# A gated feed-forward layer with quantised activations: down_w rounded by two ScalarE activations, maxima over four slots, tokens scaled in one VectorE step

## The chip, the cores and the metric

The kernel runs on one core of one Trainium2 chip. A core has five engines with a queue each, which work in order and wait for one another through semaphores: TensorE (PE in the profile, with its weight loads as PEld), VectorE (DVE), ScalarE (ACT), GpSimd (POOL) and SyncE (SP), which here issues nearly all DMAs. The metric is the device time of one execution in microseconds (us).

## The reference

The input is x (4 batches of 1024 tokens, 512 features), a condition vector per batch, norm_w, up_w (4096 x 512) and down_w (512 x 2048). Cut to what matters:

```python
scale = cond @ norm_w.T + 1.0
ms = mean(x * x, axis=-1)
h = x * (scale[:, None, :] * rsqrt(ms + EPS))
val, gate = split(h @ up_w.T, 2, axis=-1)
h = val * gelu(gate)
hq = act_quant(h)        # per token: round(h * 127 / max|h|), clipped, scaled back
wq = weight_quant(down_w)  # clip(round(w / mean|w|), -1, 1), scaled back
y = hq @ wq.T + x
```

So down_w becomes a matrix of -1, 0 and 1 with one factor, and each token of h needs the largest absolute value over all 2048 hidden features before it can be quantised.

## The kernel before

The four batches run one after the other. The 2048 hidden features are 16 blocks of 128; a batch does block j = 0 to 15, each in two halves h = 0, 1 of 512 tokens. The order of all work is written out by hand (a manual schedule), and each engine's queue follows it.

The product with up_w is done in float16 pairs (a high and a low part). In the first batch it is done plainly: `plain_half(j, h)` (lines 606 to 614) issues 12 matmuls for the gate into a PSUM bank (pg), the Gelu on ACT (L610), 12 matmuls for the value (pv, bank "E", of which there are two), and on DVE the multiplication of both into H (L614). With two banks, pv of a half can start only when L614 of the half before last has emptied its bank. The later batches use a fast product (`product`, L571) with fewer multiplications, on weights that the first batch has prepared.

So the first batch also carries, between its halves, all that prepares the rest. For each block, in `first_batch(j, sc)`: the row-wise range of up_w (`w_range`: L277, L147, L283, L286, and `w_gain` L292, on DVE), its scaling (`w_scale`, L304 on ACT), its split in two (`w_rows`: L328 on ACT, L329 on DVE, then a transposing DMA by SP), the sums of weight blocks (`s_sums`, L362 to L365 on POOL), their split (`s_high` L374 on ACT, `s_low` L378 on POOL), and the write of all this to DRAM (`s_spill`).

Three things more are spread over its blocks by small tables:

- down_w lies in R[:, 1] in eight parts of 128 x 1024. `d_sum` (ACT) has summed them, `d_total` (L437) and `d_mean` (L442 to L444, with one small matmul, pmean) make the mean and its reciprocal wsc. `d_round(n)` scales, clips to -1 and 1 and rounds part n by adding MAGIC = 1.5 * 2^23, in two DVE steps (L448, L449); `d_put(n)` takes MAGIC off again on ACT and writes fp8 (L458), and after every second part SP issues a transposing DMA (L460). `D_ROUND` says in which block.
- the tokens of the second batch (class `Tokens`, b == 1), four groups of 256 tokens, begun in blocks 6, 8, 10 and 12 (`TOKENS`): `norm` sums squares on ACT (L505), POOL makes rs (L475, L476), `scale` multiplies by rs on ACT (L513, twice) and by the condition's row sc on DVE (L518), `sums` are four POOL steps (L526 to L529). In the next block `high` (L550, ACT), `low` (L554, DVE) and `turn` (a transposing DMA, L557) follow.
- the largest absolute h per token for batch 0: `pair_max(0, i, h)` takes the maximum over blocks 2i and 2i + 1 (`tensor_reduce` over two slots, 1024 elements a partition, L700 or L705) and, but for the first pair, folds it into the running maximum (L707). `PAIRS` says in which block.

Parts of down_w, the second batch's transposed tokens and the running maxima share R: a group's `turn` writes over parts of down_w, so these must have been rounded by then.

Of the kernel before, what the change touches and what calls it, by code (L numbers as in the profile page):

```python
# [8 lines left out]
F32 = mybir.dt.float32  # L9
# [4 lines left out]
AF = mybir.ActivationFunctionType  # L14
ALU = mybir.AluOpType
# [3 lines left out]
P = 128  # L19
EXPONENT = 0x7F800000  # L20
MAGIC = 1.5 * 2.0**23
# [29 lines left out]
def glu_quant_kernel(  # L51
# [10 lines left out]
    PE, ACT, DVE, POOL, SP = nc.tensor, nc.scalar, nc.vector, nc.gpsimd, nc.sync  # L62
    B, S, D = x.shape
# [6 lines left out]
    NJ = FF // P  # L70
# [4 lines left out]
    cpool = ctx.enter_context(tc.tile_pool(name="const", bufs=1))  # L75
# [4 lines left out]
    ident = cpool.tile([P, P], F32, name="ident")  # L80
    neghalf = cpool.tile([P, 4], F32, name="neghalf")
    DVE.memset(neghalf, -0.5)
    one = cpool.tile([P, 1], F32, name="one")
    DVE.memset(one, 1.0)
    ones = one.to_broadcast([P, P])
# [36 lines left out]
    def m_view(b, h):  # L122
        return R[:, b % 2, M_AT + TOK * h : M_AT + TOK * (h + 1)]
# [16 lines left out]
    def h_slots(g, n=1):  # L140
        s = g % NSLOT
        return H[:, s : s + n]
# [73 lines left out]
    def cond_spread(dg, b0, b1, tag):  # L216
        n = b1 - b0
        pd = bank(tag, {"po": 3}.get(tag, 2), [P, B], f"pd_{b0}")[:, :n]
        PE.matmul(pd, ones[:n, :], dg, start=True, stop=True)
        return pd  # L220

    def cond_undo(pd, b0, b1):
        DVE.reciprocal(ux[:, b0:b1], pd)
        if b0 == 0:
            DVE.tensor_scalar(scT[:, :, 0], scT[:, :, 0], ux[:, 0:1], None, ALU.mult)
        DVE.tensor_copy(dx[:, b0:b1], pd)
# [40 lines left out]
    def w_load(j, ts=(1, 0)):  # L267
        if j > 2:
            SP.dma_start(out=wn(j), in_=up_v[j])
            return  # L270
        for t in ts:
            SP.dma_start(out=wn(j)[:, t], in_=up_v[j][:, t])
# [15 lines left out]
    def w_range(j, t0=0, t1=2):  # L288
        w_factor(j, w_largest(j, t0, t1), t0, t1)

    def w_gain(j):
        DVE.tensor_scalar(sg0[:, j, :], sw[:, j, :], dx[:, 0:1], None, ALU.mult)  # L292
# [63 lines left out]
    def s_sums(j):  # L356
        if j >= ROWS:
            v = wn(j).rearrange("p t (n f) -> p t n f", n=2)
            a11, a12, a21, a22 = v[:, 1, 0], v[:, 1, 1], v[:, 0, 0], v[:, 0, 1]
        else:  # L360
            a11, a12, a21, a22 = (wf(j)[:, n] for n in range(4))
        POOL.tensor_tensor(sf[:, 0], a21, a22, ALU.add)  # L362
        POOL.tensor_tensor(sf[:, 2], a11, a21, ALU.subtract)
        POOL.tensor_tensor(sf[:, 1], sf[:, 0], a11, ALU.subtract)
        POOL.tensor_tensor(sf[:, 3], a12, sf[:, 1], ALU.subtract)  # L365
# [49 lines left out]
    wsc = cpool.tile([P, 1], F32, name="wsc")  # L415
# [4 lines left out]
    def d_part(n):  # L420
        return R[:, 1, n * HF : (n + 1) * HF]

    def d_at(n):

        return n // 4 + 2 * (n % 2), n // 2 % 2, n % 2
# [9 lines left out]
    def d_total():  # L435
        part = sm.tile([P, 1], F32, name="wpart", bufs=1)
        DVE.tensor_reduce(part, wsum, AX.X, ALU.add)  # L437
        return part
# [5 lines left out]
        DVE.reciprocal(wsc, wmean)  # L444

    def d_round(n):
        dn = d_part(n)
        DVE.tensor_scalar(dn, dn, wsc, 1.0, ALU.mult, ALU.min)  # L448
        DVE.tensor_scalar(dn, dn, -1.0, MAGIC, ALU.max, ALU.add)  # L449

    tn = []

    def d_put(n):
        _, u, y = d_at(n)
        if y == 0:
            tn.append(wpool.tile([P, HF], BF16, name=f"tn_{n}", tag="v"))
        t8 = tn[-1].bitcast(F8).rearrange("p (f y) -> p f y", y=2)
        ACT.activation(t8[:, :, y], d_part(n), AF.Copy, bias=-MAGIC, saturate=False)  # L458
        if y:
            SP.dma_start_transpose(wd[:, n // 4, u], tn[-1])  # L460

# [16 lines left out]
    class Tokens:  # L478
# [31 lines left out]
        def scale(self, sc):  # L510
            xn, xt = self.xn, self.xt
            for h in range(2):
                ACT.activation(xn[:, h], xn[:, h], AF.Copy, scale=self.rs[:, h : h + 1])  # L513
                if self.b > 1:
                    POOL.tensor_tensor(xn[:, h], xn[:, h], sc, ALU.mult)
            if self.b == 1:
                s2 = sc.rearrange("p (o d) -> p o d", o=1).to_broadcast([P, 2, D])
                DVE.tensor_tensor(xn, xn, s2, ALU.mult)  # L518
            if self.b > 1:
                self.sums()  # L520

# [84 lines left out]
    def plain_half(j, h, between=nothing):  # L606
        pg = bank(*(("A", 2) if h or j == 1 else ("B", 1)), name=f"pg_{j}_{h}")
        plain(j, 1, h, pg)
        t1 = wpool.tile([P, TOK], F32, name=f"g_{j}_{h}", tag="t1")
        ACT.activation(t1, pg, AF.Gelu, scale=gain(j, 1))  # L610
        between()
        pv = bank("E", 2, name=f"pv_{j}_{h}")
        plain(j, 0, h, pv)
        DVE.scalar_tensor_tensor(h_half(j, h), pv, gain(j, 0), t1, ALU.mult, ALU.mult)  # L614
# [77 lines left out]
        z()  # L692


    def pair_max(b, i, h):

        v = h_slots(b * NJ + 2 * i, 2)[:, :, h].rearrange("p j t -> p t j")
        m = m_view(b, h)
        if i == 0:
            return [lambda: DVE.tensor_reduce(m, v, AX.X, ALU.max, apply_absolute_value=True)]  # L700
        gm = []

        def largest():
            gm.append(wpool.tile([P, TOK], F32, name=f"gm_{b}_{i}_{h}", tag="gm", bufs=1))
            DVE.tensor_reduce(gm[0], v, AX.X, ALU.max, apply_absolute_value=True)  # L705

        return [largest, lambda: DVE.tensor_tensor(m, m, gm[0], ALU.max)]  # L707
# [286 lines left out]
    def second_part():  # L994
# [8 lines left out]


    D_SUM = {0: (4, 5), 1: (6, 7), 2: (2, 3), 3: (0, 1)}
    D_ROUND = {4: (0, 1), 5: (2,), 6: (3, 4), 8: (5, 6), 10: (7,)}
    D_MEAN = min(D_ROUND)
    TOKENS = {6: 0, 8: 1, 10: 2, 12: 3}
    PAIRS = {
        3: [(0, 0), (0, 1)], 4: [(1, 0), (1, 1)], 6: [(2, 0)], 7: [(2, 1)],  # L1010
        14: [(3, 0), (3, 1), (4, 0), (4, 1)], 15: [(5, 0), (5, 1), (6, 0), (6, 1)],
    }
    toks = {}

    def next_tokens(j):

        if j in TOKENS:
            toks[j] = toks[j + 1] = Tokens(1, TOKENS[j])
            toks[j].load()
# [6 lines left out]
    def first_batch(j, sc):  # L1026

        if j + 2 <= LATE:
            w_load(j + 4)
        if j >= 4:  # L1030
            next_tokens(j + 2)
        t = toks.get(j)
        odd = t is not None and j not in TOKENS
        n = j + 2
        rows = LATE <= n < NJ
        if j + 1 < LATE:
            s_sums(j + 1)
        elif rows:
            s_sums(n)
        if j + 3 < NJ:  # L1040
            w_range(j + 3)
            w_gain(j + 3)
        if j == D_MEAN:
            part = d_total()
        plain_half(j, 0)
        if j == 3:
            pd = cond_spread(dg, 1, B, "po")
            cond_undo(pd, 1, B)
            cond_rows()
        pairs = PAIRS.get(j, ())  # L1050
        for i, h in pairs[:2]:
            for f in pair_max(0, i, h):
                f()
        if n < LATE:
            w_scale(n)
            w_rows(n)
        if j + 1 < LATE:
            s_all(j + 1)
        if t and not odd:
            t.norm()  # L1060
        for m in D_ROUND.get(j - 1, ()):
            d_put(m)
        for m in D_ROUND.get(j, ()) if j > D_MEAN else ():
            d_round(m)
        if t and not odd:
            t.scale(sc)
            t.sums()
        if j + 2 > LATE and j + 5 < NJ:
            w_load(j + 5)
        if odd:  # L1070
            t.high()
            t.low(DVE)
        if odd:
            t.turn()
        plain_half(j, 1)
        if j == D_MEAN:
            d_mean(part)
        own = rows and j + 1 >= LATE
        if own:
            s_high(n)  # L1080
            s_low(n, POOL)
        if LATE <= j + 3 < NJ:
            w_scale(j + 3)
            w_rows(j + 3)
        if own:
            s_spill(n)
        elif rows:
            s_sums(n)
            s_all(n)
            w_load(j + 5)  # L1090
        for m in D_ROUND[j] if j == D_MEAN else ():
            d_round(m)
        for i, h in pairs[2:]:
            for f in pair_max(0, i, h):
                f()
        for n in D_SUM.get(j, ()):
            d_sum(n)
        if j in (NJ - 3, NJ - 1):
            s_load_x(NJ + (j - NJ + 3) // 2)
            s_load_y(NJ + (j - NJ + 3) // 2)  # L1100
# [81 lines left out]
    for j in range(3, NJ):  # L1182
        if j == 5:
            sc = cond_load_scale(1)
# [90 lines left out]
    for b in range(1, B):  # L1275
# [5 lines left out]
        for h in range(2):  # L1281
            add_pair(
                dve, act, b - 1, last_pair, h, (0, "xz"[h]),
                lambda now, h=h: token_max(b - 1, h, am),
# [9 lines left out]
        pairs = {}  # L1294
        if b + 1 < B:
            sc = cond_load_scale(b + 1)
# [109 lines left out]
    b = B - 1  # L1406
# [159 lines left out]
```

## Time and profile before

| what | value |
|---|---|
| median of 3 runs | 735.0 us (734.93 to 735.55) |
| the profiled execution | 735.1 us |
| its span, first to last instruction | 733.3 us |
| PE busy | 721.2 us (98%) |
| DVE busy | 600.6 us (82%) |
| ACT busy | 390.9 us (53%) |
| POOL busy | 200.1 us (27%) |
| granted clock of PE | 1.00 throughout |

How to read it: the span is divided in stages with quite different loads. From 0 to about 44 us the first data come in and blocks 0 to 2 are begun; from 50.5 to 190.3 us blocks 3 to 15 of the first batch run, two halves each; after that the three other batches follow. Busy shares of the whole span say little about one stage, so the stage with the change in it has to be looked at by itself, and an engine's idle time counts only where it is on the chain that ends last. The lines of the rows are those of the kernel before.

### The profile page before, as it was taken

The page shows a single profiled execution, that of the slowest core. Times are in us where ns is not written, and L with a number is a line of the kernel's source. Part 1 is how long each engine was busy: PE and PEld are TensorE (multiplying, and loading weights), DVE is VectorE, ACT ScalarE, POOL GpSimd, SP SyncE. Part 2 cuts the span into 40 slices and gives each one's busy share as a digit, 9 for nine tenths or more (in the row PEclk, how much of TensorE's full clock was granted, in tenths as well). Part 3 has the DMA queues.
Part 4 walks back from the last instruction along what each step waited for, and adds up shares of the span by engine and source line. Part 5 has one row for each costly group of instructions (what it writes and reads, how often), then busy time and mean ns, then how long its engine had stood idle before and what let it go on. Part 6 is the DMA issues. An engine that isn't in the chain of part 4 may idle for free.

```text
span 733.3 us, 10144 instructions
## 1 busy us (share of the span) xinstructions
PE 721.2 (98%) x3661; PEld 358.5 (49%) x3661; DVE 600.6 (82%) x828; ACT 390.9 (53%) x629; POOL 200.1 (27%) x207
## 2 busy tenths in 40 slices
PE   7999999999999999999999999999999999999998
PEld 3544444444444445655444445666444444445744
DVE  6979999787898899797689887787678888755897
ACT  6868657664235675435335666453433665332274
POOL 1379867886200032450010030461020000000100
PEclk9999999999999999999999999999999999999999
DMA  6759989998344645866844646766934455452253
GB/s 239 245 176 284 275 232 237 263 260 217 116 99 103 133 107 170 180 161 173 205 101 102 123 107 173 180 145 166 227 97 105 95 110 104 102 104 91 87 188 114
DMA packets 203982, 117.30 MB, mean 160 GB/s; under 512 B 165382, under 2 KB 174487, under 8 KB 203932
## 3 DMA queue, kind: packets, MB, share of 16 engines
q1 hardware_dynamic: 203642, 116.33, 62.6%
q8 instruction: 28, 0.46, 0.3%
q10 hardware_dynamic: 290, 0.33, 0.1%
q14 instruction: 22, 0.18, 0.1%
HBM read 54.22 MB, written 23.09 MB: 105 GB/s over the span
## 4 chain that ended last, share of the span: by engine, by line
PE 84%; DVE 9%; ACT 2%; issue 2%; POOL 1%; DMA 1%; SPq 0%; DVEq 0%; ACTq 0%
PE A L571 34%; PE E L571 17%; PE B L571 8%; PE po L842 8%; PE pv L586 5%; PE pg L586 5%; PE po_end L791 4%; DVE H L614 1%; DVE H L329 1%; DVE wam L277 1%; PE po L791 1%; DVE R L448 1%; DMA H<-in_x_dram 1%; DVE gm L705 1%; DVE nx L554 1%
## 5 line engine op out<-in xcount | busy, mean ns | idle before, releaser
L571 PEld LDWEIGHTS <-SXY 128*128 128x128 f16 x2016 | 197.0, 98 | 232.5 <-issue 0.6
L571 PE MATMUL A<-R,SXY 128*128 128x512 f16 x1152 | 266.3, 379 | 0.0
L571 PE MATMUL E<-R,SXY 128*128 128x512 f16 x576 | 140.0, 379 | 0.1
L669 DVE SCALAR_TENSOR_TENSOR H<-A,sg,t 128x512 f32<-128x512 f32 x48 | 36.0, 750 | 73.2 <-PE A L571 73.1
L721 POOL PARTITION_ALL_REDUCE am<-R x8 | 14.3, 1793 | 232.0 <-DVE R L707 232.0
L763 DVE TENSOR_TENSOR H<-H,am 128x1024 f32<-128x1024 f32 x64 | 76.3, 1218 | 0.0
L586 PEld LDWEIGHTS <-SXY 128*128 128x128 f16 x486 | 47.4, 98 | 59.0 <-issue 1.7
L682 ACT ACTIVATE t<-t,sg 128x512 f32<-128x512 f32 x48 | 34.6, 721 | 70.2 <-DVE t L679 70.1
L571 PE MATMUL B<-R,SXY 128*128 128x512 f16 x288 | 70.0, 379 | 0.0
L705 DVE TENSOR_REDUCE gm<-H 128x512 f32<-128x1024 f32 x56 | 69.0, 1231 | 1.0
L586 PE MATMUL pg<-R,SXY 128*128 128x512 f16 x252 | 57.8, 379 | 0.3 <-DMA SXY<-H 0.3
L842 PE MATMUL po<-wd,R 128*128 128x256 fp8e4 (+1 forms) x448 | 56.8, 275 | 0.0
L586 PE MATMUL pv<-R,SXY 128*128 128x512 f16 x234 | 54.4, 379 | 1.1 <-DVE H L614 1.1
L842 PEld LDWEIGHTS <-R 128*128 128x128 bf16 (+1 forms) x480 | 46.9, 98 | 12.9
L666 ACT ACTIVATE t<-B,sg 128x512 f32<-128x512 f32 x48 | 33.0, 687 | 35.9 <-PE B L571 35.9
L475 POOL TENSOR_SCALAR ssq<-ssq 128x2 f32<-128x2 f32 x12 | 3.6, 299 | 176.7 <-ACT xt L505 124.1
L649 ACT COPY t<-A 128x512 f32<-128x512 f32 x48 | 27.9, 582 | 39.8 <-PE A L571 39.5
L657 ACT COPY B<-A 128x512 f32<-128x512 f32 x48 | 27.5, 572 | 39.0 <-PE A L571 38.6
L771 ACT ACTIVATE H<-H 128x1024 f32<-128x1024 f32 x38 | 39.9, 1050 | 14.2 <-DVE H L763 14.1
L661 ACT COPY v<-E 128x512 f32<-128x512 f32 x48 | 28.1, 585 | 31.6 <-PE E L571 27.8
L707 DVE TENSOR_TENSOR R<-R,gm 128x512 f32<-128x512 f32 x56 | 41.8, 747 | 1.3
L688 DVE SCALAR_TENSOR_TENSOR H<-v,sg,t 128x512 f32<-128x512 f32 x48 | 36.6, 762 | 7.4 <-ACT t L682 7.4
(206 smaller groups left out, 992.7 us busy)
## 6 DMA issues: line engine op xcount, KB each, us to landing
SXY<-s_dram SPq DMA_DIRECT2D x57, 256.0 KB, 3.1
s_dram<-SXY SPq DMA_DIRECT2D x18, 384.0 KB, 3.2
H<-in_L_cond_up_w_dram SPq DMA_DIRECT2D x13, 512.0 KB, 5.1
SXY<-s_dram SPq DMA_DIRECT2D x39, 128.0 KB, 3.2
xr<-in_x_dram SPq DMA_DIRECT2D x19, 256.0 KB, 3.1
out_dram<-xr SPq DMA_DIRECT2D x19, 256.0 KB, 2.5
H<-in_x_dram SPq DMA_DIRECT2D x8, 512.0 KB, 7.6
R<-in_L_cond_down_w_dram SPq DMA_DIRECT2D x8, 512.0 KB, 6.7
```

The costliest lines, as they stand in the source:

```text
L571: PE.matmul(o, s[:, w, k, :], tv[:, :, c, l, k, :], start=start and n == 0, stop=stop and n == len(TERMS) - 1, skip_group_check=True,)
L586: PE.matmul(ps, a[k // 2][:, w, k % 2, :], XP[:, l, k, h * TOK : (h + 1) * TOK], start=n == 0, stop=n == len(terms) - 1,)
L666: ACT.activation(cur["t1"], pb, AF.Gelu, scale=gain(g, 1))
L669: DVE.scalar_tensor_tensor(h_half(g - 1, 0), prev["A"], gain(g - 1, 0), prev["t1"], ALU.mult, ALU.mult)
L682: ACT.activation(prev["t2"], prev["t2"], AF.Gelu, scale=gain(g - 1, 1))
L688: DVE.scalar_tensor_tensor(h_half(g - 1, 1), prev["v"], gain(g - 1, 0), prev["t2"], ALU.mult, ALU.mult)
L705: DVE.tensor_reduce(gm[0], v, AX.X, ALU.max, apply_absolute_value=True)
L707: return [largest, lambda: DVE.tensor_tensor(m, m, gm[0], ALU.max)]
L763: DVE.tensor_tensor(v, v, r.to_broadcast([P, 2, TOK]), ALU.mult)
L771: ACT.activation(v, v, AF.Copy, bias=MAGIC)
L791: PE.matmul(po.rearrange("p (y c o) -> p y c o", c=2, o=P), q[:, a, h, j], wd8[:, :, j // n, j % n, :, y0:y1].rearrange("p c o y -> p y c o"),
L842: PE.matmul(po, w[:, j], m, start=start and j == 0, stop=stop and j == n - 1, skip_group_check=True,)
```

## The change

It has three parts, all within the first batch:

1. `d_round` becomes one ACT activation (Copy with scale wsc and bias MAGIC, which rounds), and `d_put` uses the function Sign with bias -MAGIC in place of Copy, which maps the rounded integer to -1, 0 or 1. Both stand together in the half before the second one of a block; the parts are spread over blocks 5, 6, 7, 9, 10, 11 and 12. A constant tile `unmagic` is set at the start.
2. For the second batch, `Tokens.scale` no longer uses ACT: DVE does `(x * rs) * sc` in one step for each of the two rows.
3. `pair_max` can take several pairs at once; three of the four calls for each half now reduce over four slots (2048 elements a partition), and the table `LARGEST` has one call in a block.

```diff
+    unmagic = cpool.tile([P, 1], F32, name="unmagic")
+    DVE.memset(unmagic, -MAGIC)
...
     def d_round(n):
         dn = d_part(n)
-        DVE.tensor_scalar(dn, dn, wsc, 1.0, ALU.mult, ALU.min)
-        DVE.tensor_scalar(dn, dn, -1.0, MAGIC, ALU.max, ALU.add)
+        ACT.activation(dn, dn, AF.Copy, scale=wsc, bias=MAGIC)
...
-        ACT.activation(t8[:, :, y], d_part(n), AF.Copy, bias=-MAGIC, saturate=False)
+        ACT.activation(t8[:, :, y], d_part(n), AF.Sign, bias=unmagic, saturate=False)
...
             for h in range(2):
-                ACT.activation(xn[:, h], xn[:, h], AF.Copy, scale=self.rs[:, h : h + 1])
-                if self.b > 1:
+                r = self.rs[:, h : h + 1]
+                if self.b == 1:
+                    DVE.scalar_tensor_tensor(xn[:, h], xn[:, h], r, sc, ALU.mult, ALU.mult)
+                else:
+                    ACT.activation(xn[:, h], xn[:, h], AF.Copy, scale=r)
                     POOL.tensor_tensor(xn[:, h], xn[:, h], sc, ALU.mult)
-            if self.b == 1:
-                s2 = sc.rearrange("p (o d) -> p o d", o=1).to_broadcast([P, 2, D])
-                DVE.tensor_tensor(xn, xn, s2, ALU.mult)
...
-    def pair_max(b, i, h):
+    def pair_max(b, i, h, pairs=1):
-        v = h_slots(b * NJ + 2 * i, 2)[:, :, h].rearrange("p j t -> p t j")
+        v = h_slots(b * NJ + 2 * i, 2 * pairs)[:, :, h].rearrange("p j t -> p t j")
...
-    D_ROUND = {4: (0, 1), 5: (2,), 6: (3, 4), 8: (5, 6), 10: (7,)}
-    D_MEAN = min(D_ROUND)
+    D_ROUND = {5: (0, 1), 6: (2,), 7: (3,), 9: (4,), 10: (5,), 11: (6,), 12: (7,)}
+    D_MEAN = 4
-    PAIRS = {
-        3: [(0, 0), (0, 1)], 4: [(1, 0), (1, 1)], 6: [(2, 0)], 7: [(2, 1)],
-        14: [(3, 0), (3, 1), (4, 0), (4, 1)], 15: [(5, 0), (5, 1), (6, 0), (6, 1)],
+    LARGEST = {
+        4: (0, 0, 2), 5: (0, 1, 2), 8: (2, 0, 2), 10: (2, 1, 2), 12: (4, 0, 2), 13: (4, 1, 2),
+        14: (6, 0, 1), 15: (6, 1, 1),
     }
...
-        pairs = PAIRS.get(j, ())
-        for i, h in pairs[:2]:
-            for f in pair_max(0, i, h):
+        if j in LARGEST:
+            for f in pair_max(0, *LARGEST[j]):
                 f()
...
-        for m in D_ROUND.get(j - 1, ()):
+        for m in D_ROUND.get(j, ()):
+            d_round(m)
             d_put(m)
-        for m in D_ROUND.get(j, ()) if j > D_MEAN else ():
-            d_round(m)
...
-        for m in D_ROUND[j] if j == D_MEAN else ():
-            d_round(m)
-        for i, h in pairs[2:]:
-            for f in pair_max(0, i, h):
-                f()
```

On the queues: PE's and POOL's keep their order; DVE's has 23 instructions fewer (16 rounding steps, 4 token steps, 6 reductions and 6 maxima go, 8 token steps and one constant come), ACT's has as many as before (8 rounding steps come, 8 token steps go); on SP's the third transposing DMA of down_w moves back from block 9 to block 10 and the fourth from block 11 to block 12. ACT's queue holds two table loads before and after.

## The prediction

> **What bounds the kernel now.** First the engine totals and the chain that ended last, on the page:
>
> ```profile
> PE 721.2 (98%) x3661; PEld 358.5 (49%) x3661; DVE 600.6 (82%) x828; ACT 390.9 (53%) x629; POOL 200.1 (27%) x207
> PE 84%; DVE 9%; ACT 2%; issue 2%; POOL 1%; DMA 1%; SPq 0%; DVEq 0%; ACTq 0%
> ```
>
> PE is idle for only 733.3 - 721.2 = 12.1 us, and no matmul is removed, so nothing can bring more than that. DVE's 9% of the chain says that it holds PE up somewhere. So next the busy time by stage (columns: stretch, length, busy us of PE, PEld, DVE, ACT, POOL, PE's clock, DMA share, GB/s):
>
> ```profile
> 44.00:72.00 28.00, 27.53 (x128) 12.17 (x126) 22.76 (x32) 24.40 (x41) 24.69 (x25) 1.00 0.87 257
> 72.00:132.00 60.00, 56.46 (x260) 25.43 (x261) 58.09 (x75) 38.21 (x61) 46.83 (x48) 1.00 0.95 250
> 132.00:190.00 58.00, 58.00 (x270) 26.30 (x269) 45.89 (x55) 31.64 (x53) 39.11 (x40) 1.00 0.90 226
> ```
>
> From 72 to 132 us (blocks 5 to 10) DVE is full (58.1 of 60) and PE loses 3.5 us, while ACT has 21.8 us free; from 132 to 190 PE loses nothing. Then PE's timeline there (start, duration, idle before and its releaser):
>
> ```profile
> 69.11 2.75 PE L586 MATMUL pv<-R,SXY 128*128 128x512 f16 x12
> 72.64 0.38 PE L442 MATMUL pmean<-wpart,one 128*128 128x1 f32 x2 [0.78 <-DVE wpart L437]
> 72.89 2.75 PE L586 MATMUL pg<-R 128*128 128x512 f16 x12
> ...
> 83.24 2.75 PE L586 MATMUL pg<-R,SXY 128*128 128x512 f16 x12
> 86.74 2.75 PE L586 MATMUL pv<-R,SXY 128*128 128x512 f16 x12 [0.74 <-DVE H L614]
> ...
> 110.11 2.75 PE L586 MATMUL pg<-R 128*128 128x512 f16 x12
> 114.64 2.75 PE L586 MATMUL pv<-R 128*128 128x512 f16 x12 [1.78 <-DVE H L614]
> ...
> 127.59 2.75 PE L586 MATMUL pg<-R,SXY 128*128 128x512 f16 x12
> 130.72 2.75 PE L586 MATMUL pv<-R,SXY 128*128 128x512 f16 x12 [0.38 <-DVE H L614]
> ```
>
> An undisturbed group of 12 follows the last after 2.59 us. So the pv of halves (6,0), (8,1) and (10,0) start 0.91, 1.94 and 0.54 us late, the group at 107.52 another 0.07: 3.46 us, all but the 0.07 behind L614 on DVE, which has to empty the bank "E" of two halves earlier. The step from 69.11 to 72.89 is 3.78, of which 2.59 are the group and 0.25 pmean itself: 0.94 us of waiting for wpart. Together 4.40 us. How late DVE is: L614 of (5,0) starts at 85.94, 7.7 us after its pv group ended (75.47 + 2.75).
>
> **What the change takes from DVE's queue.** Prices from its groups:
>
> ```profile
> L448 DVE TENSOR_SCALAR R<-R,wsc 128x1024 f32<-128x1024 f32 x8 | 6.8, 854 | 0.0
> L449 DVE TENSOR_SCALAR R<-R 128x1024 f32<-128x1024 f32 x8 | 7.7, 961 | 0.3
> L458 ACT ACTIVATE tn<-R 128x1024 fp8e4<-128x1024 f32 x8 | 8.2, 1051 | 5.6 <-DVE R L449 5.6
> L705 DVE TENSOR_REDUCE gm<-H 128x512 f32<-128x1024 f32 x56 | 69.0, 1231 | 1.0
> ```
>
> Rounding: 6.8 + 7.7 = 14.5 us go. Token scaling: four L518 of 1.22 go (4.9); eight steps of 128x512 with two SBUF inputs come. Their form is not in the first batch; the nearest row is L910 (same operation, SBUF only, 0.68), the far one a 128x512 subtraction beside a busy POOL (L554, 1.07). I take 0.70: 5.6 us come, between 5.4 and 8.6. Maxima: two reductions (2 x 1.23) and one L707 (0.69 in this stage) become one reduction over 2048 elements. No row has it; from 1024 elements (L277, 1.21) to 1536 (L190, 1.76) is 1.07 ns an element, so 1.76 + 0.55 = 2.30. Bounds: 1.76, the shorter reduction, and 2.46, two single ones. I take 2.30: 0.85 saved, six times, 5.1 us. Net 14.5 + 4.9 - 5.6 + 5.1 = 18.9 us off DVE, most of it before 132 us, where it was late.
>
> Stall by stall, with DVE's queue carried forward. (6,0): between L614 of (4,0) at 72.51 and that of (5,0) at 85.94 stood two reductions with maxima (73.17 to 77.03, 3.86), now one of 2.30, and four rounding steps (79.62 to 84.17, 4.55), now none. So L614 of (5,0) could run 6.1 us earlier, at 79.8; PE needs it done by 85.8. The stall goes whole, with over 5 us to spare. (8,1): before L614 of (7,1) at 113.85 another 2.7 + 2.8 us of rounding and two reductions with maxima, 1.9 each, go, one reduction of 2.30 comes, 7.0 us less (the token step about even). With the 6.1 that is more than the whole lateness; DVE then waits for PE and ACT. (10,0): 2.8 us of rounding go, 2.30 + 0.69 come in block 8, about even on a queue now in step. After that an even block costs DVE: L329 1.7, L277 1.2, small steps 1.0, two L614 1.4, reduction and maximum 3.0, scaling 1.4, so 9.7 of PE's 10.36 us; an odd one 1.7 + 1.2 + 1.0 + 1.4 with L554's 2.6 (up to 4.7 beside POOL), 7.9 to 10.0. Tight, but the two banks forgive 7 us.
>
> wpart: the two reductions at 61.54 go (2.4 us), but the L329 behind them needs ACT's L328, which ended at 66.73, so the queue gains only 66.93 - 66.75 = 0.18 us. Then come small steps that last 0.2 us alone and 0.7 to 1.7 beside a POOL step; slipping in front of one would free the whole 0.94. I take 0.3, nearer the low end.
>
> **What it adds to ACT.** Eight roundings of the size of L458 (1.05, or 1.15 if a pointer scale costs what L513 at 0.72 costs over L505 at 0.62) come, 8.4 to 9.2 us; eight L513, 5.7 us, go. The net 2.7 to 3.5 us is covered by 21.8 + 26.4 us of idle ACT between 72 and 190. Largest single place: four activations in block 5, 4.2 us in front of Gelu (5,1). They start when Gelu (5,0) is done (77.5); wsc is then ready, about 76. They end at 81.7, that Gelu at 82.4, L614 of (5,1) at 83 to 84.5; its bank is needed at 90. Were that cover gone, each us of ACT would be one of PE.
>
> The Trainium skill, "ScalarE: Activation LUTs", section "Rules for kernel authors", speaks against this: multiply, min and max belong on VectorE, not ScalarE. The rows agree on one step (L448 took 0.75 us undisturbed, L458 takes 1.05), and by the rule alone eight of them would cost 8 x 0.30 = 2.4 us, 737.4; but DVE needs two steps for what ACT does in one, and here the dearer engine is the idle one.
>
> **Moved waits.** L513 waited 14.4 us for POOL's rs (four times, up to 3.9); now DVE waits for rs, and L614 (j,1), L329 and L277 stand behind it. In block 6 I carry rs to about 91.0 (95.03 before, as ACT's L374 is no longer behind L458's waits) and DVE to 91.1; L614 (6,1) has until 100. In blocks 8, 10 and 12 the reduction runs first and rs is there. On SP the two later down_w transposes now wait for blocks 10 and 12; behind them stand the next up_w load and the token transpose. The loads run two blocks ahead, so an added us there is hidden by some 20. unmagic's memset is hidden behind the first x loads.
>
> **The sum.** 3.46 + 0.3 = 3.76 us off the profiled execution: span 729.5, with its 1.8 us around it 731.3; against the median (735.0) 731.2. From 130.72 on the chain is PE alone, so it reaches the end. All of 4.40 gives 730.6; with 0.5 us of new small waits and nothing at wpart 732.0.
>
> **Rivals.** *POOL sets the pace of blocks 10 to 13.* There L614 was also barely in time: of (11,0) it ended at 151.3 for a pv at 151.44. Behind it stood L329, L328, L374 and POOL's sums, and POOL's round of two blocks took 143.85 to 164.23, 20.4 us against PE's 20.7. If that chain doesn't move forward, PE runs into it and keeps only its 0.1 to 0.6 us of slack: about 734.5, no change. Against: POOL's waits for L518 (15.6 us in four) were themselves DVE's lateness; in block 6 its sums come at about 92.5 instead of 101.3.
>
> *The wide reduction is dear.* In blocks 8, 10, 12 it stands ahead of the scaling for which POOL waits. With r its price, POOL's round is 17.7 of work and r + 1.75 of waiting; over 20.7 it falls behind by r - 1.27, three times, and 7.0 are forgiven. At 2.30 that is 3.1 and free. From r = 4.9 the stalls outweigh the 3.76; at 6.9 they are 9.9, and the time is 741. For it: no row shows four slots. Against: the slope above.
>
> *Sign does not do what it says cheaply*: with a table of its own ACT would load 16 times 1.28 us (the row of L1001), 20.5 us. Against: the built program still has two loads. *DMA*: at 0.95 busy it could give back some 0.5 us in 72 to 132; that is inside the range.
>
> **Numbers.** Forecast 0.76, with 730.5 to 732.6; POOL's pace 0.13; wide reduction 0.06; others 0.05. Under 0.2% (1.5 us) this kernel's measurement can't be told from no change. The range is 730.4 to 733.8. Faster 0.80 (forecast and part of POOL's case), same 0.13, slower 0.07.
>
> **What would show it.** PE idle between 72 and 190 near zero, with L614 within 3 us of its pv group in blocks 5 to 9; reduction rows near 2.3 us; two table loads; ACT some 3 us busier. Wrong if PE waits for L614 in blocks 10 to 13, or if a row L518 or L705 runs over 4 us.

## The result and the profile after

The changed kernel takes 734.06 us (median of 20 runs, 730.90 to 735.91), the kernel before 736.09 in 20 runs beside it; the ratio is 0.9968 with an interval of 0.9957 to 0.9979. By the ratio it is faster by some 2.4 us, by the two medians by 2.0; the forecast was 3.8. The profiled execution took 733.24 us with a span of 731.4. The totals of the engines and the chain that ended last:

```profile
PE 720.9 (99%) x3661; PEld 358.9 (49%) x3661; DVE 587.2 (80%) x805; ACT 396.1 (54%) x629; POOL 195.8 (27%) x207
PE 87%; DVE 4%; POOL 4%; DMA 2%; ACT 1%; issue 1%; SPq 0%; POOLq 0%; DVEq 0%; ACTq 0%
```

DVE lost 13.4 us where 18.9 were forecast, ACT gained 5.2, and POOL's share of the chain rose from 1% to 4% though its work fell. The same stages as before (columns as there):

```profile
72.00:132.00 60.00, 60.00 (x281) 27.34 (x280) 51.98 (x60) 45.25 (x70) 49.27 (x52) 1.00 0.98 264
132.00:190.00 58.00, 56.27 (x260) 25.23 (x259) 47.44 (x52) 29.89 (x46) 32.93 (x36) 1.00 0.85 214
```

From 72 to 132 us PE is now full: the 3.5 us of before have come back. But from 132 to 190, where it lost nothing, it now loses 1.7. PE's timeline shows where (start, duration, idle before and its releaser):

```profile
69.54 2.75 PE L588 MATMUL pv<-R,SXY 128*128 128x512 f16 x12
72.13 0.28 PE L444 MATMUL pmean<-wpart,one 128*128 128x1 f32 x2
72.27 2.75 PE L588 MATMUL pg<-R 128*128 128x512 f16 x12
...
155.15 2.75 PE L588 MATMUL pg<-R,SXY 128*128 128x512 f16 x12
158.00 2.75 PE L588 MATMUL pv<-R,SXY 128*128 128x512 f16 x12
160.59 2.75 PE L588 MATMUL pg<-R,SXY 128*128 128x512 f16 x12
164.39 2.75 PE L588 MATMUL pv<-R,SXY 128*128 128x512 f16 x12 [1.05 <-DVE H L616]
...
172.16 2.75 PE L588 MATMUL pg<-R 128*128 128x512 f16 x12
175.49 2.75 PE L588 MATMUL pv<-R 128*128 128x512 f16 x12 [0.58 <-DVE H L616]
```

(L616 is the L614 of before; most lines have moved by two.) At the undisturbed pitch of 2.59 the pv groups of (13,0), (13,1) and (14,1) come 0.26, 1.21 and 0.74 us late, 2.21 together. The three old stalls are gone, and so is the wait for wpart: the step from 69.54 to 72.27 is 2.73, it was 3.78.

To compare kernels I use the *stage*: from the first matmul of block 3 (50.46 us before, 50.88 after) to the first matmul of the second batch (190.29, 188.43). It was 139.83 us and is 137.55, so 2.28 less; the rest of the span is 543.0 to 543.1 in every run here, and the part before the stage depends on the execution (50.4 to 53.8). A stage is that of one profiled execution: two executions of the changed kernel gave 137.55 and 138.25, so a difference of less than some 0.7 us between two stages says little.

The new waits point to DVE's groups of four slots (count | busy, mean ns | idle), in blocks 4 to 15 of the changed kernel:

```profile
L707 DVE TENSOR_REDUCE gm<-H 128x512 f32<-128x2048 f32 x4 | 15.0, 3752 | 0.0
L702 DVE TENSOR_REDUCE R<-H 128x512 f32<-128x2048 f32 x2 | 7.5, 3772 | 0.0
```

3.77 us each, not 2.30. What this does to POOL is seen in its four steps L528, the first of each token group's sums:

```profile
93.63 0.73 POOL L528 TENSOR_TENSOR xt<-xn 128x256 f32<-128x256 f32 x1 [3.34 <-DVE xn L517]
117.02 0.73 POOL L528 TENSOR_TENSOR xt<-xa 128x256 f32<-128x256 f32 x1 [5.72 <-DVE xa L517]
140.38 0.73 POOL L528 TENSOR_TENSOR xt<-xn 128x256 f32<-128x256 f32 x1 [5.73 <-DVE xn L517]
163.75 0.72 POOL L528 TENSOR_TENSOR xt<-xa 128x256 f32<-128x256 f32 x1 [5.74 <-DVE xa L517]
```

A round of two blocks takes 23.4 us (117.02 to 140.38), while PE does two blocks in 8 x 2.59 = 20.72. The chain that ended last runs around this round (start, length, what; pieces of it from one round):

```profile
115.54 1.42 DVE xa L517 x2
...
120.88 1.64 POOL SXY L380
...
125.90 1.60 POOL H L367
...
127.83 1.34 ACT H L306 x2
129.20 1.05 ACT H L330
130.28 1.23 DVE H L331
...
133.94 0.65 DVE H L616
134.59 3.67 DVE gm L707
...
138.89 1.42 DVE xn L517 x2
```

DVE scales the tokens, POOL sums them and only then does the weights' sums of two blocks, ACT's L376 waits for these with L306 and L330 behind it in the queue, DVE's L331 waits for L330, and the wide reduction stands between L331 and the next scaling. In a queue that works in order this is a loop, and PE is not in it until it runs into L616.

### The profile page after: what moved, and what is told of

Same layout as the page of the kernel before. It is cut to its first block, busy times and chain, and to the rows that moved or that the text cites. A ratio compares the mean times of both kernels' runs of the same rounds, so it can differ in the third digit from the quotient of the medians.

```text
span 731.4 us, 10126 instructions
## 1 busy us (share of the span) xinstructions
PE 720.9 (99%) x3661; PEld 358.9 (49%) x3661; DVE 587.2 (80%) x805; ACT 396.1 (54%) x629; POOL 195.8 (27%) x207
## 4 chain that ended last, share of the span: by engine, by line
PE 87%; DVE 4%; POOL 4%; DMA 2%; ACT 1%; issue 1%; SPq 0%; POOLq 0%; DVEq 0%; ACTq 0%
PE A L573 34%; PE E L573 17%; PE B L573 8%; PE po L844 8%; PE pg L588 6%; PE pv L588 6%; PE po_end L793 4%; DVE gm L707 1%; PE po L793 1%; DMA H<-in_x_dram 1%; POOL xt L529 1%; DMA SXY<-H 1%; POOL H L367 1%; PE po_B L844 0%; POOL R L380 0%
## 5 line engine op out<-in xcount | busy, mean ns | idle before, releaser
L707 DVE TENSOR_REDUCE gm<-H 128x512 f32<-128x1024 f32 (+1 forms) x50 | 71.6, 1433 | 0.8
L777 ACT ACTIVATE R<-H 128x1024 bf16<-128x1024 f32 x38 | 40.1, 1055 | 0.8
```

The costliest lines, as they stand in the source:

```text
L777: ACT.activation(q, by_tile(v), AF.Copy, bias=-MAGIC)
```

## The experiments

Three theories. **A**: the loop just shown; the reduction matters because it stands ahead of the scaling, once in each round. **B**: the roundings on ACT make the Gelus, and with them L616, late. **C**: DVE simply has too much to do from block 10 on, wherever it stands. A table first; "waits" is PE's idle time behind L616 (or L614) as its timeline prints it, "first sums" is the first L528 counted from the stage's start, "round" a third of the time from the first L528 to the fourth.

| kernel | ratio to before (interval) | stage, us | waits | first sums | round |
|---|---|---|---|---|---|
| before | 1 | 139.83 | 2.90 | 50.8 | 20.98 |
| changed | 0.9968 (0.9957 to 0.9979) | 137.55 | 1.63 | 42.8 | 23.37 |
| after_again | 0.9970 (0.9956 to 0.9983) | 138.25 | 2.42 | 43.5 | 23.36 |
| e1_split | 0.9944 (0.9927 to 0.9962) | 137.08 | 1.42 | 44.2 | 22.98 |
| e2_scale_first | 0.9943 (0.9927 to 0.9959) | 135.34 | 0 | 43.3 | 20.22 |
| e2_again | 0.9941 (0.9921 to 0.9962) | 135.34 | 0 | 43.7 | 20.22 |
| e3_old_maxima | 0.9950 (0.9935 to 0.9965) | 136.40 | 0 | 46.7 | 19.31 |
| p1_rounding | 0.9953 (0.9936 to 0.9971) | 136.39 | 0 | 45.7 | 20.51 |
| p2_tokens | 1.0011 (0.9998 to 1.0024) | 140.06 | 2.94 | 51.1 | 20.57 |
| p3_maxima | 1.0107 (1.0082 to 1.0132) | 147.86 | 8.28 | 49.6 | 24.53 |
| d1_more_before | 1.0035 (1.0019 to 1.0052) | 143.74 | 5.98 | 43.8 | 24.76 |
| d2_more_behind | 0.9985 (0.9975 to 0.9996) | 139.05 | 3.21 | 42.9 | 23.12 |
| u2_tokens_undone | 0.9962 (0.9947 to 0.9978) | 136.50 | 0.85 | 42.7 | 23.03 |

### Each maximum by itself (e1_split)

The changed kernel, with each reduction over four slots taken as two over two slots, in the same place:

```diff
-            for f in pair_max(0, *LARGEST[j]):
-                f()
+            i, h, n_pairs = LARGEST[j]
+            for i in range(i, i + n_pairs):
+                for f in pair_max(0, i, h):
+                    f()
```

> The changed kernel with each reduction over four slots made as two reductions over two slots and their maximum, in the same places. Theory A (the round DVE scaling, POOL sums, ACT, DVE paces blocks 8 to 13, and the wide reduction of 3.77 us in front of the scaling is what stretches it to 23.4 us): reduction and maximum together fall from 3.77 + 0.69 to 2 x 1.23 + 2 x 0.69 = 3.84, four times 0.62 before block 14, 2.5 us of lateness; PE's 2.2 us of waiting in blocks 13 and 14 shrink to 0 to 0.5, the time by about 1.9 us, ratio to before near 0.994. Theory B (ACT's added roundings make the Gelu late): no change, ratio 0.997.

Two waits of PE are left:

```profile
159.62 2.75 PE L588 MATMUL pv<-R,SXY 128*128 128x512 f16 x12 [0.90 <-DVE H L616]
165.49 2.75 PE L588 MATMUL pv<-R,SXY 128*128 128x512 f16 x12 [0.52 <-DVE H L616]
```

The ratio of 0.9944 is what was expected. By the stage more was expected: it gains only 0.5 us on the changed kernel. Its pairs with their folds cost 2 x 1.23 + 2 x 0.69 = 3.84 against 3.75 + 0.69 = 4.44, so the round is only 0.4 to 0.6 shorter and still above 20.72. And it starts later. In block 6 DVE waits for the condition's row, which comes by DMA, at 91.51 - 51.71 = 39.8 us of the stage in this execution:

```profile
91.51 0.49 DVE L248 TENSOR_SCALAR sc<-sc,ux 128x512 f32<-128x512 f32 x1 [2.95 <-DMA sc<-rows_dram]
```

In the changed kernel that step starts at 89.23 - 50.88 = 38.35. These 1.4 us are the later first sums of the table. What such a delay costs is seen in the second execution of the changed kernel (after_again):

```profile
92.07 0.49 DVE L248 TENSOR_SCALAR sc<-sc,ux 128x512 f32<-128x512 f32 x1 [2.38 <-DMA sc<-rows_dram]
```

There it starts at 92.07 - 53.01 = 39.06, that is 0.71 later, the rounds are the same, and the stage is 0.70 longer. At this rate the 1.4 us account for the rest of e1's gain (0.5 + 1.4 = 1.9, as expected). Why the row comes later in one execution than in another is not shown.

### Scaling ahead of the maxima (e2_scale_first, e2_again)

The same instructions as the changed kernel; only the maxima stand behind the token scaling and its sums:

```diff
-        if j in LARGEST:
-            for f in pair_max(0, *LARGEST[j]):
-                f()
         if n < LATE:
...
             t.sums()
+        if j in LARGEST:
+            for f in pair_max(0, *LARGEST[j]):
+                f()
```

> The changed kernel with the maxima issued after the token scaling of the same block instead of before it; the wide reduction stays. Theory A: POOL's wait for the scaling falls from 5.7 us to under 2, its round to under 20.7, PE waits nowhere in blocks 8 to 15; 2.2 us gained over the changed kernel, ratio to before near 0.994. Theory C (DVE simply has too much in the even blocks, whatever the order): DVE's work is the same, so the waits stay, ratio 0.997. Theory B: no change either.

```profile
94.14 0.72 POOL L528 TENSOR_TENSOR xt<-xn 128x256 f32<-128x256 f32 x1 [3.88 <-DVE xn L517]
113.29 0.73 POOL L528 TENSOR_TENSOR xt<-xa 128x256 f32<-128x256 f32 x1 [1.53 <-DVE xa L517]
134.08 0.73 POOL L528 TENSOR_TENSOR xt<-xn 128x256 f32<-128x256 f32 x1 [2.26 <-DVE xn L517]
154.80 0.73 POOL L528 TENSOR_TENSOR xt<-xa 128x256 f32<-128x256 f32 x1 [2.26 <-DVE xa L517]
```

These are POOL's waits of this kernel: 5.7 has become 1.5 to 2.3 (under 2 was expected), and the rounds of 20.79 and 20.72 are PE's own pace. In its PE timeline no group from 51 us to the end of the stage waits at all. The stage is 135.34, that is 2.21 less than in the changed kernel and just the 2.21 of its late groups. DVE does exactly as much as before the move, so C can't be the whole story; the order is.

It was run a second time, beside the changed kernel and on one chip with it:

> The changed kernel itself, on the same chip as the next three. Theory A: PE waits about 2.2 us in blocks 13 and 14 again; ratio to before 0.996 to 0.998.

> The changed kernel with the maxima behind the token scaling, beside the changed kernel on one chip. Theory A: 2.2 us or 0.3% under it, no wait of PE in blocks 4 to 15; ratio to before 0.993 to 0.995. Theories B and C: the same as the changed kernel.

731.72 against 733.55 us, the stage again 135.34. In after_again PE waits 0.79, 1.04 and 0.59 at the places seen above. This kernel beats both: 4.3 us off the kernel before (0.0059 x 736) with the change's own instructions.

### The old maxima with the other two parts (e3_old_maxima)

The changed kernel with the table `PAIRS` of before and its two loops in place of `LARGEST`.

> The changed kernel with the maxima as before the change (two slots each, in blocks 3, 4, 6, 7, 14 and 15). Theories A and C: nothing in front of the scaling in blocks 8, 10 and 12, no waits in 8 to 15, 2.2 us gained; the two reductions in block 3 are back in front of wpart, which may give back up to 0.9: ratio to before 0.994 to 0.9955. Theory B: no gain over the changed kernel, 0.997 or above.

PE doesn't wait behind L616 at all, its only idle time in blocks 4 to 15 is again 0.79 us for wpart, and the stage is 136.40: 1.15 less than with the new maxima. So part 3, as it stands, costs more than it brings by the stage (the intervals of the two ratios still overlap); the 1.06 by which e2's stage is shorter than this one is what part 3 is worth in the right place, and it is the wpart wait.

### The prices by themselves (prices)

> A kernel that computes nothing of the reference: it loads x, runs single instructions on VectorE and ScalarE three times each and writes x out. For the prices alone, with POOL idle. If a reduction costs by the element, four slots take 2.3 us and the layout does not matter; if the 3.77 us of the changed kernel are the price of groups of four, packed groups of four cost the same; if they come from the distance of 1024 elements between the slots, groups of four packed, 512 or 1032 apart are cheaper; if they come from what runs beside it there, four slots take 2.3 here.

Six of DVE's groups (line, shapes, count | busy, mean ns | idle). L63 to L66 are 2, 3, 4 and 6 slots 1024 elements apart; L69 is groups of four packed side by side, L70 four elements 512 apart:

```profile
L66 DVE TENSOR_REDUCE o<-X 128x512 f32<-128x3072 f32 x3 | 16.0, 5331 | 0.1
L65 DVE TENSOR_REDUCE o<-X 128x512 f32<-128x2048 f32 x3 | 10.9, 3645 | 0.1
L70 DVE TENSOR_REDUCE o<-F 128x512 f32<-128x2048 f32 x3 | 10.9, 3618 | 0.1
L69 DVE TENSOR_REDUCE o<-F 128x512 f32<-128x2048 f32 x3 | 6.9, 2286 | 0.1
L64 DVE TENSOR_REDUCE o<-X 128x512 f32<-128x1536 f32 x3 | 5.7, 1912 | 0.1
L63 DVE TENSOR_REDUCE o<-X 128x512 f32<-128x1024 f32 x3 | 3.7, 1228 | 0.1
```

From two slots to three the slope is (1912 - 1228) / 512 = 1.34 ns an element, from three to four (3645 - 1912) / 512 = 3.4. The 2.30 of the prediction is right for four elements that lie side by side (2.29), and wrong for four that lie apart (3.65), at 512 as at 1024 elements. With POOL idle in this kernel and no one to wait for, 3.65 of the 3.77 us are the instruction itself and not a collision. Two reductions over two slots and one maximum (2 x 1.23 + 0.69 = 3.15) are cheaper than the one that replaced them.

### Each part alone (p1_rounding, p2_tokens, p3_maxima)

The kernel before with part 1, part 2 or part 3 of the change alone.

> The kernel before with the first part of the change alone (rounding on ACT and its table of blocks); maxima and token scaling as before. If the rounding is what made DVE late: 14.5 us less on DVE, the three late value products (3.46 us) gone, the wait for wpart (0.94) still there, no waits in blocks 10 to 15; ratio 0.995 to 0.996. If the change needs all three parts to free DVE, or ACT's load (scaling and rounding both) makes the Gelu late: waits of 1 us and more remain, ratio 0.998 or above.

> The kernel before with the third part alone (maxima by the new table, wide reductions). Theory A with the measured 3.77 us: the wait for wpart goes (0.9 gained), but DVE, late as before from the rounding, gets 3.77 us more in block 5 and 4.46 in blocks 8, 10 and 12 and gives back only 1.9 in 6 and 7: 3 to 8 us of new waits, ratio 1.003 to 1.010. If the maxima over four slots were the relief that the kernel needed: below 1.

> The kernel before with the second part alone. DVE, late in blocks 6 and 8, pays 0.2 us more each time and does not wait for rs; in blocks 10 and 12 POOL's wait for the scaled tokens shortens by about 1.2 us, but PE waits for nothing there: within 0.5 us of the kernel before, ratio 0.9993 to 1.0007 if the measurement can show it. If waiting for rs on DVE holds up the value products: 1.003 or above.

Part 1 alone gives a stage of 136.39 us, 3.44 less than before and better than the whole change (by the ratios, 0.9953 and 0.9968, the two can't be told apart). All three old stalls are gone, and this is the only idle time of PE left in blocks 4 to 15:

```profile
72.80 0.38 PE L444 MATMUL pmean<-wpart,one 128*128 128x1 f32 x2 [0.78 <-DVE wpart L439]
```

With B, the 16 activations should have shown behind the Gelus; nothing waits there. Part 2 alone can't be told from no change. Part 3 alone makes the stage 8.03 us longer, a little more than was expected: it has the wide reductions and still has the rounding steps on DVE, so POOL's round is 24.53, and PE waits in eight places. Some 3 of the 8 us are PE's clock after the longest of these waits (see the last section).

### One more reduction, ahead or behind (d1_more_before, d2_more_behind)

The changed kernel with one more reduction over two slots (1.23 us, its output unused) in blocks 8, 10 and 12. In d1 it stands behind the maxima and ahead of the scaling; in d2 the same lines stand behind `t.sums()`:

```diff
+        if j in (8, 10, 12):
+            extra = wpool.tile([P, TOK], F32, name=f"extra_{j}", tag="gm", bufs=1)
+            v = h_slots(j - 2, 2)[:, :, 0].rearrange("p j t -> p t j")
+            DVE.tensor_reduce(extra, v, AX.X, ALU.max, apply_absolute_value=True)
```

> The changed kernel with one reduction over two slots more (1.23 us, its result unused) between the maxima and the token scaling of blocks 8, 10 and 12. Theory A (what stands in front of the scaling goes into the round one to one): the round of two blocks goes from 23.4 to 24.6, PE's waits in blocks 12 to 14 from 2.2 to about 5.9, the time 3.7 us above the changed kernel, ratio near 1.002. Theory C (load of DVE): the same 3 x 1.23 us, wherever they stand, so the next run should show the same time as this.

> The same extra reduction behind the token scaling of the same blocks. Theory A: it falls into the 2.6 us for which DVE waits for ACT's cast two halves later, POOL's sums start when they did, and the time is that of the changed kernel within 0.5 us, ratio 0.996 to 0.998. Theory C: like the run before, near 1.002.

```profile
121.56 0.73 POOL L528 TENSOR_TENSOR xt<-xa 128x256 f32<-128x256 f32 x1 [7.00 <-DVE xa L517]
```

POOL's wait in d1 is 7.00, 1.28 more than the 5.72 of the changed kernel: the added reduction, unhidden, once a round. PE's waits rise from 1.63 to 5.98, and the ratio of 1.0035 (1.0019 to 1.0052) is a little above the 1.002 expected. In d2 POOL's round doesn't grow (23.12), as A says. But PE waits twice:

```profile
164.67 2.75 PE L588 MATMUL pv<-R,SXY 128*128 128x512 f16 x12 [1.65 <-DVE H L616]
176.75 2.75 PE L588 MATMUL pv<-R 128*128 128x512 f16 x12 [1.56 <-DVE H L616]
```

So the stage is 1.50 longer than in the changed kernel, and that is more than was expected of a reduction that nobody on the loop waits for. Where DVE is already at the limit, L616 stands behind whatever is in its queue, so C holds that much: a reduction behind the loop costs about its own length once (1.5 us by the stage, 0.0015 x 736 = 1.1 by the ratio), one within the loop is paid in every round. By the stage that is 6.19, but the execution in the profile was the longest of ten: 1.69 of it are PE's clock (see the last section), and its first sums came 1.0 later, so about 3.5 are left for three reductions of 1.23.

### Part 2 undone (u2_tokens_undone)

The changed kernel with `Tokens.scale` as before: two activations on ACT and one step L520 on DVE.

> The changed kernel with the second part undone (scaling by rs on ACT again, by sc on DVE in one step of 1.22 us, behind the wide reduction). Theory A: DVE's step is 0.2 us shorter than the two new ones of 1.41 together and ACT is through with its two long before the reduction ends, so the round shortens by 0.2 and the time is that of the changed kernel or up to 0.6 us less; ratio 0.996 to 0.998. Theory B (ACT is the tight engine): 1.3 us more of ACT in front of four Gelus, slower by 1 us or more, ratio above 0.998.

The ratio is that of the changed kernel within the intervals, and PE waits 0.85 where it waited 1.63. ACT is busy 5.1 us more here (401.2 against 396.1) without harm, which is a second sign against B, and part 2 brings nothing: in its round two DVE steps of 0.74 stand where one of 1.22 did. The same comes from e3 and p1, which differ by part 2 alone: their stages are 136.40 and 136.39, their ratios 0.9950 and 0.9953.

## Why the prediction was right and wrong

**The old stalls.** They went whole, as forecast, at all three places. L616 of (5,0) ran at 81.34 where 79.8 was forecast, and PE took its bank over at 85.22 without a wait; the reduction before it was 1.5 longer. p1 shows that part 1 alone does this: the 14.5 us of rounding steps taken off DVE.

**ACT.** Rounding and Sign took 1.14 and 1.15 us where 1.05 or 1.15 were given; the four in block 5 ended at 81.4 (81.7 forecast), no table load was added, and the cover held. ACT's total rose by 5.2 us rather than 2.7 to 3.5. The Sign steps with their pointer bias also cost 0.1 more each than the copies they replace, which makes 9.1 + 0.8 - 5.7 = 4.2; the other 1.0 doesn't show in these rows. The rule of the Trainium skill that was weighed ("ScalarE: Activation LUTs", "Rules for kernel authors": multiply, min and max on VectorE) would have kept the rounding off ACT; p1 runs 0.9953 (0.9936 to 0.9971) against it. The rule compares one engine's step with the other's, and here the idle time beside the step decided.

**wpart.** 0.3 was taken, 0.94 was the upper bound, and 1.05 came (the small product pmean itself took 0.14 in place of 0.25). The small step in question is L292 before and L294 after:

```profile
70.87 1.66 DVE L292 TENSOR_SCALAR sg<-sw,dx 128x2 f32<-128x2 f32 x1
```

```profile
70.69 0.21 DVE L294 TENSOR_SCALAR sg<-sw,dx 128x2 f32<-128x2 f32 x1
```

POOL's L378 started at 70.86 before, just ahead of the first; its L380 started at 70.77 after, just behind the second. Counted from the start of the stage, the step came 0.60 us earlier (19.81 for 20.41) and POOL's 0.51 earlier (19.89 for 20.40), so that DVE was now first by 0.08. Of the 0.60, 0.15 are the earlier start of L331 (0.18 was forecast); the rest is that L331 took 1.27 in place of 1.72, which was not in the forecast. It comes from part 3: p1 and e3 still wait, e2 and the changed kernel don't. That 0.09 us of difference decided over 1 us is more luck than forecast.

**The step that failed** is a term of the sum: one reduction over 2048 elements at 2.30 us, with bounds of 1.76 and 2.46. It measured 3.77. The slope behind it came from two rows (L277, L190) that reduce elements side by side, not four slots 1024 apart, and the upper bound of two single reductions was taken for a limit that it isn't. So DVE lost 0.62 us more with each wide reduction than with the three steps it replaced, where 0.85 was to be saved.

**The mechanism was named, its size was not.** The second rival had the loop: POOL's round at 17.7 of work and r + 1.75 of waiting, together r + 19.45. At r = 3.77 that is 23.2, and 23.37 was measured. By its own account it then fell behind by 3 x 2.5 = 7.5 with 7.0 forgiven, so 0.5 us of stalls. The 7.0 was the second term of wrong size: PE was in fact at its limit after two rounds, 2 x (23.37 - 20.72) = 5.3, less the first 0.26 of delay, so some 5.0 are forgiven. The third round cost the other 1.95. A part of this is a wait that the prediction had left out: in block 6 DVE stood idle for 1.67 us behind the condition's row (L248), and the two executions of the changed kernel show that a later start of the loop goes into the stage (0.71 us later, 0.70 us longer). So the 3.46 + 0.3 that were counted on became 3.46 + 1.05 - 2.21 = 2.30; the stage shows 2.28. One of the signs that the prediction set for being wrong came: PE waits in blocks 13 and 14, for L616 of blocks 12 and 13. The other, a reduction of over 4 us, did not: it was set too high, for 3.77 us already cost PE 2.21 us.

The first rival, POOL's pace, had about 734.5, close to what was measured, but that is luck. It needed POOL's chain not to move forward, and the first sums came at 42.8 us of the stage instead of 50.8; what held PE up was the longer round.

**The time.** 734.06 lies 0.3 us above the range. The kernel before measured 736.09 in the 20 runs beside it, 1.1 above the median of three that the forecast started from, so that a part of the miss in the time is that of its starting point. The failed term shows in the gain: the direction held, but it was 2.4 in place of 3.8.

## What to carry to other kernels

Where an engine in one stage does work for a loop of other engines, the order in its queue can matter as much as its load: put what the loop waits for first, and the wide work behind it (here 2.2 us with the same instructions). Before several steps are merged into one wider one, measure the wide one with its real strides; a slope from narrower or packed rows doesn't carry. And run the parts of a change alone: here, by the stage, one part brought more than the whole, one nothing, and one was a loss that its neighbour had covered.

## What the runs showed of the hardware

**A reduction over strided groups of four or six** cost some 1.75 ns an element in the run prices (3645 / 2048, 5331 / 3072), over packed groups of four 1.12 (2286 / 2048), over strided pairs 1.20 (1228 / 1024) and threes 1.25 (1912 / 1536). The distance (512 or 1024) made next to no difference (3618 and 3645).

**A wait of PE can cost more than itself.** In p3, twelve matmuls after an idle time of 3.31 us took nearly twice their 2.75:

```profile
128.10 5.28 PE L586 MATMUL pv<-R,SXY 128*128 128x512 f16 x12 [3.31 <-DVE H L614]
```

The windows of that run show that PE's granted clock, the figure after the five engines, had fallen to half:

```profile
130.00:132.00 2.00, 2.00 (x6) 0.71 (x5) 1.90 (x5) 0.62 (x1) 1.92 (x3) 0.50 0.83 154
```

In d1 an idle time of 2.27 us left the group after it at 2.75, and one of 2.30 made it 4.44:

```profile
146.84 2.75 PE L588 MATMUL pv<-R 128*128 128x512 f16 x12 [2.27 <-DVE H L616]
...
171.85 4.44 PE L588 MATMUL pv<-R,SXY 128*128 128x512 f16 x12 [2.30 <-DVE H L616]
```

The granted clock of d1 from 172 to 174 us was 0.54. So the length of the idle time alone didn't decide here. The Trainium skill, "TensorE: Matmul & The Clock Gate", asks for no idle gap over about 3 us (section "Why this matters for your kernels") and describes a free-running window of some 3.4 us (section "What's actually happening"). p3 agrees with the first, and d1 shows a gap of 2.30 that lost the clock all the same; no run here shows the window itself. A loss of clock was also seen at the start of an execution: in after_again PE idled 2.88 us before the first transposes of x, these took 3.40 us, and the clock from 12 to 16 us was 0.58. In the changed kernel's first profile it idled 1.77, they took 1.97, and the clock stayed at 1.00. It is a part of why the start varies between executions of one kernel, and none of the stage's figures above contains it but those of p3 and d1.
